# Pinning a DRAM clearing among a GNN layer's loads, and issuing the next layer's edge gathers behind the expert scatters

## The chip, the cores and the metric

The kernel runs on one core of a Trainium2 chip. The metric is device time in microseconds (us) of one execution, the median of several. The engines are named as the profile names them: PE (TensorE, matmuls, with its weight loads as PEld), DVE (VectorE), ACT (ScalarE), POOL (GpSimd) and SP (SyncE, which here only issues DMAs). SPq and ACTq are the DMA issues of SP and ACT.

## The reference, cut to what matters

A graph of 3125 nodes with 256 features and 100,000 edges sorted by `dst` passes through two layers:

```
xn = layernorm(x)
x  = x + gnn0(xn, edges) + linear_attention0(xn)      # layer 0: two rounds of (x + mean of neighbours) @ W
x  = x + moe0(layernorm(x))                           # 8 experts, each node goes to its top 2
xn = layernorm(x)
x  = x + relational_attention(xn, edges, edge_type)   # layer 1: softmax over each node's edges
       + linear_attention1(xn)
x  = x + moe1(layernorm(x))                           # 6 experts, top 2
```

The change touches two pieces of preparation. The first is the table into which the tokens of `moe0` are sorted by expert, and which must hold zeros where no token comes. The second is the reading of the edge lists (`dst`, `src`, `edge_type`) in the order in which layer 1 wants them.

## The kernel before

The work goes through these stages, with times of the profiled execution:

- **Start (0 to 75 us).** `x` is loaded by ACT's queue (`xs`). `Places` (L919) finds where each window of edges begins: it makes row numbers `wrow_i` (L954), gathers 400 KB of `dst` rows six times through two buffers `rw` (L958), and counts in each on DVE (L960). `Windows` (L982) gathers ten windows of 128 KB (`win_dst`, `win_src`, L994) and turns them into the classes `val_a` and `val_s`.
- **Counts (75 to 368 us).** `Counts` (L1604) builds the adjacency matrix of edge counts in DRAM, in 79 groups: one-hots `oh_a` and `oh_s` on DVE (L1619), matmuls (L1634), a cast to `adj_o` on ACT (L1635, six buffers), and a store by SP (L1636, 250 KB from 125 partitions). The linear attention of layer 0 is woven in by hand.
- **Two GNN layers (375 to 925 us).** For each group of columns (512 nodes, the last ones smaller) five loads `at` of the adjacency (L2169, 640 KB each, four buffers, SP's queue) feed the matmuls of L2180. After a group of the second layer, `Routes.tokens` (L1821) picks the two experts of each node, computes the rows `slot` on DVE (L1905), and POOL scatters the nodes' rows into the DRAM table `route_x` (L1909), two DMAs for each tile of 128 nodes, 50 in all.
- **Experts (964 to 1500 us).** `experts` (L1974) takes 32 steps: 8 for the first 256 rows of each expert and 24 for what is left over. Each step loads 256 rows `fx` from `route_x` (L1993) and the weights, transposes (`ftp`, L2013), scales on DVE (`fxe`, L2015), multiplies (`fhp`, L2030; `fyp`, L2038) and stores `route_y`. After each step it calls `beside(s)`, in which other work is placed between the steps.
- **Layer 1 (1500 us to the end).** A table of projected rows is written, then 831 gathers from it feed the attention over edges, and the last experts follow.

Two things stand beside these stages. `Routes.clear` (L1815) writes zeros over `route_x`: 104 DMAs of 256 KB by SP, from a tile `zero`. In the program's text it is called four DMAs at a time after each `at` load of the first GNN layer, from its second group on:

```
for _ in range(4 if layer == 0 and c else 0):
    next(clear, None)
```

`Blocks` (L1030) prepares the edges of layer 1: 75 gathers on POOL (L1048, 25 each for `dst`, `src` and `edge_type`, each 128 rows of 34 numbers), and then `finish`, a generator of steps, the first of which reads `dst`, the second `rel`, the third `rel` and `src`. `beside(s)` takes one of these steps after each expert step from step 8 on, and starts the load of `wn` (L2243, eight DMAs on POOL's queue) at step 16, for the first use at step 22.

The order of instructions on an engine is not always that of the text. A scheduler places them, and where an instruction's inputs are ready early it may be moved ahead. In stretches under `manual_schedule` the text's order holds: in the counts for all engines, in the experts only for the engines in `ORDERED` (L916: PE, DVE and ACT). SP and POOL are not in it. So, in this kernel, SP's queue holds 68 clears ahead of the first adjacency store and the other 36 among the first stores, and POOL's queue holds 14 of the edge gathers ahead of the four scatters of the 23rd and 24th tile, and 17 more between these and the two scatters of the last, the 25th.

`tc.keep_in_program_order(ins)` ties an instruction behind everything written before it for its engine, as an order of issue; it adds no wait.

Of the kernel before, what the change touches and what calls it, by code (L numbers as in the profile page):

```python
# [9 lines left out]
I32 = mybir.dt.int32  # L10
# [7 lines left out]
P = 128  # L18
NB = 25
# [389 lines left out]
def run_all(steps):  # L409
    for _ in steps:  # L410
        pass
# [493 lines left out]
BO = [sum(BW[:b]) for b in range(NB + 1)]  # L905
# [124 lines left out]
class Blocks:  # L1030
# [3 lines left out]
    def __init__(self, nc, keep, dram, pool, a, places):  # L1034
        k = lambda shape, dt, name: keep.tile(shape, dt, name=name)
        t = lambda shape, dt, name: pool.tile(shape, dt, name=name)
        n = BO[NB]
        self.at = k([P, n], I32, "b_at")
        self.dl = k([P, n], F32, "b_dl")
        self.rel = k([P, n], BF, "b_rel")  # L1040
        self.found = k([P, 1], F32, "b_found")
        self.order = dram.tile([n, P], BF, name="b_order")
        self.raw = raw = {}
        for name, src in (("dst", "dst"), ("src", "src"), ("rel", "edge_type_8")):
            raw[name] = t([P, n], I32, "b_" + name)
            flat = a[src].rearrange("(e o) -> e o", o=1)
            for b in range(NB):
                nc.gpsimd.indirect_dma_start(  # L1048
                    out=raw[name][:, BO[b]:BO[b + 1]], out_offset=None, in_=flat,
                    in_offset=bass.IndirectOffsetOnAxis(ap=places.blocks[:, b:b + 1], axis=0))  # L1050

    def finish(self, nc, C, dram, pool, ps):

# [81 lines left out]
class Layer1:  # L1135
# [50 lines left out]
    def load(self, A, c):  # L1186

        if c >= A["n"]:
            return
        k = min(CW, A["w"] - c * CW)  # L1190
        i = A["c0"] + c * CW
        oe = self.wk.tile([P, CW * P], BF, name="oe", bufs=3)
        self.nc.sync.dma_start(oe[:, :k * P], self.B.order[i:i + k, :].rearrange("c e -> (c e)")[None, :]
                               .to_broadcast([P, k * P]))
        A["oe"][c] = oe
# [596 lines left out]
class Routes:  # L1792
# [19 lines left out]
        nc.vector.memset(self.ones, 1.0)  # L1812
        self.tiles = t([1, 2, NT], I32, "route_tiles")

    def clear(self, nc, z):  # L1815

        for i in range(0, NE0 * XR, 2 * P):
            nc.sync.dma_start(self.x[i:i + 2 * P, :].rearrange("(p a) d -> p (a d)", p=P), z)  # L1818
            yield

    def tokens(self, tc, C, wk, ps, xs, t0, nt, wr, br):  # L1821
# [223 lines left out]
def score_weights(nc, C, a, late, f, wn, blk_p):  # L2045

    at_w = f.tile([P, 2, 2 * HD], F32, name="at_w")
    head = f.tile([P, 2, HD], F32, name="head")
    for oc in range(2):
        nc.vector.tensor_scalar(head[:, oc, :], C.row[:, :HD], float(-4 * oc), C.pd[DH],  # L2050
                                op0=OP.add, op1=OP.is_equal)
    for i, name in enumerate(("L1_gnn_attn_srcc", "L1_gnn_attn_dstc")):
        col = f.tile([P, 2], F32, name=f"att{i}")
        nc.sync.dma_start(col, a[name])
        for oc in range(2):
            nc.vector.tensor_scalar(at_w[:, oc, i * HD:(i + 1) * HD], head[:, oc, :],
                                    col[:, oc:oc + 1], None, op0=OP.mult)

    score_w = late.tile([P, 2, 2 * R * HD], F32, name="score_w")
    sp = blk_p.tile([P, 2, R, 2 * HD], F32, name="sp", tag="w")  # L2060
    for r in range(R):
        for k in range(2):
            for oc in range(2):
                nc.tensor.matmul(sp[:, k, r, :], wn[:, r, oc, k * P:(k + 1) * P], at_w[:, oc, :],
                                 start=(oc == 0), stop=(oc == 1))
    for k in range(2):
        nc.vector.tensor_copy(score_w[:, k, :R * HD].rearrange("p (r h) -> p r h", r=R),
                              sp[:, k, :, :HD])
        nc.vector.tensor_copy(score_w[:, k, R * HD:].rearrange("p (h r) -> p r h", r=R),
                              sp[:, k, :, HD:])  # L2070
    return score_w
# [3 lines left out]
def fast(ctx: ExitStack, tc: tile.TileContext, a, out, flag):  # L2075
    nc = tc.nc
# [14 lines left out]
    T_ = Routes(nc, C, keep, dram)  # L2091
# [8 lines left out]
    zero = nodes.tile([P, 2 * D], F32, name="zero")  # L2100
    nc.vector.memset(zero, 0.0)
    nc.scalar.dma_start(gam, row_bc(a["L0_mix_gamma"], D))
    with tc.tile_pool(name="a_sb", bufs=1) as a_sb, tc.tile_pool(name="a_ps", bufs=2, space=PSUM) as a_ps, \
# [3 lines left out]
        with tc.tile_pool(name="find", bufs=1) as find:  # L2107
            places = Places(nc, C, keep, find, a_ps, a)
# [34 lines left out]
    with tc.tile_pool(name="g", bufs=1) as g1, tc.tile_pool(name="ga", bufs=4) as ga, \  # L2143
# [4 lines left out]
        br = g1.tile([P, NE0], F32, name="br")  # L2148
        nc.scalar.dma_start(br, row_bc(a["L0_ffn_br"], NE0))
        rdeg = g1.tile([P, NP], F32, name="rdeg")  # L2150
        clear = T_.clear(nc, zero)
        for t in range(0, NB, 2):
            mix.result(t, mix_p, gt, gam, xs)
        py = nodes.tile([P, 3, NB, D], BF, name="py", tag="late")
# [1 line left out]
        for layer, parts in enumerate((px, py)):  # L2156
# [5 lines left out]
            for c, cw in (GROUPS if layer == 0 else GROUPS1):  # L2162
                agg = [gg.tile([P, 512], F32, name=f"agg{g}") for g in range(2)]
                sums = rdeg[:, c:c + cw]
                for kb in range(NB // KB):
                    at = ga.tile([P, KB, 512], BF, name="at")
                    k0 = kb * KB
                    m = KB if k0 + KB < NB else KB - 1
                    nc.sync.dma_start(at[:, :m, :cw], adj[k0 * P:(k0 + m) * P, c:c + cw].rearrange(  # L2169
                        "(k p) s -> p k s", p=P))  # L2170
                    if m < KB:
                        nc.sync.dma_start(at[:LAST, m, :cw], adj[full:N, c:c + cw])
                    for _ in range(4 if layer == 0 and c else 0):
                        next(clear, None)
                    for i in range(KB):
                        k = k0 + i
                        n = P if k < NB - 1 else LAST
                        for g in range(2):
                            for j in range(3):
                                nc.tensor.matmul(agg[g][:, :cw], parts[j][:n, k, g * P:(g + 1) * P],  # L2180
                                                 at[:n, i, :cw], start=(k == 0 and j == 0),
                                                 stop=(k == NB - 1 and j == 2))
                        if layer == 0 and k > 0:
                            nc.vector.tensor_tensor(sums[:n, :], at[:n, i, :cw],
                                                    at[:n, 0, :cw] if k == 1 else sums[:n, :], OP.add)
# [25 lines left out]
                for i in range(nt):  # L2211
                    t = c // P + i
                    z = gt.tile([P, D], F32, name="z")
# [17 lines left out]
    with tc.tile_pool(name="blk", bufs=1) as blk, tc.tile_pool(name="blk_p", bufs=1, space=PSUM) as blk_p, \  # L2231
            tc.tile_pool(name="f", bufs=1) as f:
        B_ = Blocks(nc, late, dram, blk, a, places)

        score_w = None
        wn = f.tile([P, R, 2, D], F32, name="wn")
        steps = B_.finish(nc, C, dram, blk, blk_p)

        def beside(s):
            nonlocal score_w  # L2240
            if s == 16:
                for r in range(R):
                    nc.gpsimd.dma_start(wn[:, r], a["L1_gnn_W"][r].rearrange("(k p) n -> p k n", p=P))  # L2243
            if s == 22:
                score_w = score_weights(nc, C, a, late, f, wn, blk_p)
            if s >= 8:
                next(steps, None)
            if s < NE0 + NT - 1:
                return
            run_all(steps)  # L2250

            ok = blk.tile([P, 1], F32, name="ok")
            nc.vector.memset(ok, 1.0)
            tot = blk_p.tile([1, 1], F32, name="tot", tag="w")
            nc.tensor.matmul(tot, found_w, ok, start=True, stop=False)
            nc.tensor.matmul(tot, B_.found, ok, start=False, stop=True)
            nc.vector.tensor_scalar(flag, tot, float(2 * E), None, op0=OP.not_equal)

        T_.results(nc, C, blk)
        with tc.tile_pool(name="fw", bufs=2) as fw, tc.tile_pool(name="fk", bufs=3) as fk, \  # L2260
                tc.tile_pool(name="fp", bufs=2, space=PSUM) as fp:
            with tc.manual_schedule(engines=ORDERED):
                experts(tc, C, T_, a, f, fw, fk, fp, beside)


    with tc.tile_pool(name="n1", bufs=1) as n1:
# [7 lines left out]
        with tc.tile_pool(name="r", bufs=1) as r1, tc.tile_pool(name="rw", bufs=3) as rw, \  # L2274
# [21 lines left out]
            for t in range(NB):  # L2296
                for i in range(2):
                    y = rw.tile([P, D], F32, name=f"y{i}")
                    nc.gpsimd.indirect_dma_start(  # L2299
                        out=y, out_offset=None, in_=T_.y,  # L2300
                        in_offset=bass.IndirectOffsetOnAxis(ap=T_.back[:, i * NB + t:i * NB + t + 1], axis=0))
# [22 lines left out]
                ap = rp.tile([P, 2 * R * HD], F32, name="ap", tag="b")  # L2324
# [8 lines left out]
                n = P if t < NB - 1 else LAST  # L2333
# [34 lines left out]
@with_exitstack  # L2368
def gps_two_layers(ctx: ExitStack, tc: tile.TileContext, a, out):
    nc = tc.nc  # L2370
    hold = ctx.enter_context(tc.tile_pool(name="hold", bufs=1))
    flag = hold.tile([1, 1], I32, name="flag")
    fast(tc, a, out, flag)
    with tc.If(nc.values_load(flag[0:1, 0:1], min_val=0, max_val=1) > 0):
        general(tc, a, out)
# [51 lines left out]
```

## Time and profile before

| | us |
|---|---|
| median of 3 runs | 3091.99 |
| lowest and highest | 3090.39, 3094.61 |
| the profiled execution's own time | 3668.28 |
| its span in the profile | 3666.3 |
| PE busy in the span | 2620.8 (71%) |
| DVE busy | 1834.4 (50%) |
| POOL busy | 1061.8 (29%) |
| ACT busy | 738.1 (20%) |

The profiled execution is slower than the others by 576 us, so its span is not the metric, and stretches of it have to be carried over with care. A line of the profile names the engine, the line of the kernel, the operation and the tiles (`out<-in`); the idle time of the engine just before, and what ended it, stand in square brackets in a timeline. A row of a table of windows has the stretch, its length, then for PE, PEld, DVE, ACT and POOL the busy time and the number of instructions, the clock granted to PE, the mean busy share of the 16 DMA engines and the GB/s that they moved. DMA issues on SP, ACT and POOL end with the issue; the data lands later.

### The profile page before, as it was taken

The page shows a single profiled execution, that of the slowest core. Times are in us where ns is not written, and L with a number is a line of the kernel's source. Part 1 is how long each engine was busy: PE and PEld are TensorE (multiplying, and loading weights), DVE is VectorE, ACT ScalarE, POOL GpSimd, SP SyncE. Part 2 cuts the span into 40 slices and gives each one's busy share as a digit, 9 for nine tenths or more (in the row PEclk, how much of TensorE's full clock was granted, in tenths as well). Part 3 has the DMA queues.
Part 4 walks back from the last instruction along what each step waited for, and adds up shares of the span by engine and source line. Part 5 has one row for each costly group of instructions (what it writes and reads, how often), then busy time and mean ns, then how long its engine had stood idle before and what let it go on. Part 6 is the DMA issues. An engine that isn't in the chain of part 4 may idle for free.

```text
span 3666.3 us, 38085 instructions
## 1 busy us (share of the span) xinstructions
PE 2620.8 (71%) x13535; PEld 1774.6 (48%) x13535; DVE 1834.4 (50%) x4049; ACT 738.1 (20%) x1637; POOL 1061.8 (29%) x1040
## 2 busy tenths in 40 slices
PE   2787999998189999799454337637736746845778
PEld 1565545456178888444233324434424533533556
DVE  6898877565111111476315444454545544544552
ACT  3444121222022222232100011111101101101122
POOL 1000000012710000310324644644543554554500
PEclk9899999999589999899776668968867877977989
DMA  8533322332256656443423333433432342343322
GB/s 297 153 84 74 93 84 77 97 98 85 66 171 191 188 170 186 154 144 126 147 71 82 104 94 98 117 90 98 114 100 78 104 123 83 106 123 84 105 58 82
DMA packets 382414, 421.67 MB, mean 115 GB/s; under 512 B 143878, under 2 KB 316044, under 8 KB 381958
## 3 DMA queue, kind: packets, MB, share of 16 engines
q1 hardware_dynamic: 311680, 270.61, 24.4%
q0 software_dynamic: 49072, 132.49, 13.0%
q10 hardware_dynamic: 21462, 16.03, 1.4%
q8 instruction: 109, 1.79, 0.2%
q14 instruction: 91, 0.75, 0.1%
HBM read 321.04 MB, written 97.96 MB: 114 GB/s over the span
## 4 chain that ended last, share of the span: by engine, by line
PE 50%; another core or an unknown queue 18%; DVE 15%; issue 8%; DMA 4%; ACT 2%; POOL 2%; SPq 1%; ACTq 0%; DVEq 0%; POOLq 0%
PE agg L2180 8%; PE fhp L2030 6%; PE fyp L2038 6%; PE sums L1468 6%; PE hp L2318 5%; PE hp L1270 4%; PE yp L1322 3%; DVE r L1454 2%; PE hp L2202 1%; DVE oh_a L1619 1%; DVE oh_s L1619 1%; SPq L1818 1%; PE cnt L1634 1%; PE kvp L2336 1%
## 5 line engine op out<-in xcount | busy, mean ns | idle before, releaser
L1383 POOL DMA_INDIRECT r<-tab,b_at x831 | 865.8, 1042 | 1049.5 <-PE tp L1524 472.1
L1468 PE MATMUL sums<-r,oh 128*128 128x264 f32 x1662 | 436.5, 420 | 78.5 <-DVE oh L1457 60.0
L1214 PE MATMUL dp<-a,ot 128*128 128x64 bf16 x2493 | 116.5, 210 | 485.6 <-DVE own L1225 320.7
L1468 PEld LDWEIGHTS sums<-r,oh 128*128 128x128 f32 x1662 | 343.3, 209 | 165.5 <-issue 60.3
L1214 PEld LDWEIGHTS <-ot 128*128 128x128 bf16 x2493 | 108.3, 109 | 512.6 <-issue 416.1
L1909 POOL DMA_INDIRECT route_x<-x,slot x50 | 50.4, 1007 | 802.1 <-DVE slot L1905 649.7
L1225 DVE TENSOR_TENSOR own<-dp,orel 128x512 f32<-128x512 f32 (+1 forms) x122 | 74.1, 607 | 401.7 <-remote 331.9
L2030 PE MATMUL fhp<-fxe,fw 128*128 128x256 f32 x1024 | 239.3, 392 | 45.6 <-issue 19.2
L1454 DVE TENSOR_TENSOR r<-r 128x1792 f32<-128x1792 f32 (+2 forms) x123 | 240.5, 1955 | 0.0
L2030 PEld LDWEIGHTS fhp<-fxe,fw 128*128 128x128 f32 x1024 | 189.7, 195 | 89.0 <-issue 21.5
L1322 PE MATMUL yp<-ew,h 128*128 128x256 f32 x600 | 168.2, 431 | 89.0 <-DVE xs L1326 86.4
L1273 ACT ACTIVATE h<-hp,bc 128x512 f32<-128x512 f32 (+2 forms) x168 | 105.4, 639 | 622.2 <-PE hp L1270 322.8
L2038 PE MATMUL fyp<-fw,fhid 128*128 128x256 f32 x1024 | 228.0, 381 | 0.0
L2180 PE MATMUL agg<-at,py 128*128 128x512 bf16 (+4 forms) x1200 | 219.6, 336 | 1.4 <-issue 1.3
L2180 PE MATMUL agg<-at,px 128*128 128x512 bf16 (+2 forms) x1050 | 217.6, 358 | 0.8 <-DMA row_b<-in_L_gnn_b 0.8
L2038 PEld LDWEIGHTS fyp<-fw,fhid 128*128 128x128 f32 x1024 | 193.4, 191 | 25.3
L2299 POOL DMA_INDIRECT y<-route_y,slot x50 | 50.0, 1001 | 509.1 <-DMA wq<-in_L_mix_wqT 481.7
L2318 PE MATMUL hp<-wt,xt 128*128 128x512 f32 x400 | 184.4, 609 | 12.1 <-ACT stage L2323 6.0
L2031 ACT ACTIVATE fhid<-fhp,fb 128x256 f32<-128x256 f32 x256 | 121.3, 474 | 324.0 <-PE fhp L2030 280.3
L1322 PEld LDWEIGHTS yp<-ew,h 128*128 128x128 f32 x600 | 124.5, 216 | 127.2 <-DVE xs L1326 96.5
L1270 PE MATMUL hp<-xt,ew 128*128 128x512 f32 (+2 forms) x336 | 165.6, 617 | 17.5 <-ACT h L1273 11.6
L1270 PE MATMUL hp<-h,ew 128*128 128x512 f32 (+2 forms) x336 | 159.6, 601 | 1.5 <-issue 1.5
(419 smaller groups left out, 3834.6 us busy)
## 6 DMA issues: line engine op xcount, KB each, us to landing
fw<-in_L_ffn_W SPq DMA_DIRECT2D x64, 1024.0 KB
ew<-in_L_ffn_expert_w SPq DMA_DIRECT2D x126, 256.0 KB
at<-adj SPq DMA_DIRECT2D x44, 640.0 KB
route_x<-zero SPq DMA_DIRECT2D x104, 256.0 KB
tab<-stage SPq DMA_DIRECT2D x25, 1056.0 KB
oe<-b_order SPq DMA_DIRECT2D x97, 256.0 KB
adj<-adj_o SPq DMA_DIRECT2D x78, 250.0 KB
r<-tab,b_at POOLq DMA_INDIRECT x831
```

Source lines behind the costliest of these rows:

```text
L1214: nc.tensor.matmul(dp[:, i, :, :].rearrange("p h r -> p (h r)"), ot[:, i * P:(i + 1) * P], A["a3"][:, j, :], start=(j == 0), stop=(j == 2))
L1270: nc.tensor.matmul(hp[:, :W], ws[i, e][:, n, j * P:(j + 1) * P], x[:, n, :W], start=(n == 0), stop=(n == 1))
L1273: nc.scalar.activation(o[:, j, :W], hp[:, :W], AF.Relu, bias=b[:, e, j:j + 1])
L1322: nc.tensor.matmul(yp, h2[e][:, n, i * P:(i + 1) * P], ws[3, e][:, n, :], start=(n == 0), stop=(n == 1))
L1383: st = self.nc.gpsimd.indirect_dma_start(out=r[:, c, :], out_offset=None, in_=self.table, in_offset=bass.IndirectOffsetOnAxis(ap=self.B.at ...
L1454: nc.vector.tensor_tensor(rv, rv, r[:, :k, D:, None].to_broadcast([P, k, HD, DH]), OP.mult)
L1468: mm = nc.tensor.matmul(self.sums, oh[:, c, :], r[:, c, :], start=(i == 0), stop=(i == w - 1))
L2030: nc.tensor.matmul(hp, w1[:, k, i * P:(i + 1) * P], xe[:, k, :], start=(k == 0), stop=(k == 1))
L2031: nc.scalar.activation(hid[:, i, :], hp, AF.Gelu, bias=b1[:, 0, i:i + 1])
L2038: nc.tensor.matmul(yp, hid[:, i, t * P:(t + 1) * P], w2[:, i, :], start=(i == 0), stop=(i == K1 - 1))
L2180: nc.tensor.matmul(agg[g][:, :cw], parts[j][:n, k, g * P:(g + 1) * P], at[:n, i, :cw], start=(k == 0 and j == 0), stop=(k == NB - 1 and j ...
L2318: nc.tensor.matmul(hp.rearrange("p r d -> p (r d)"), xt[:, k, :], wt[:, k, j * 512:(j + 1) * 512], start=(k == 0), stop=(k == 1))
```

## The change

- `Routes.clear` issues its DMAs with `keep_in_program_order`, so that they stay among the `at` loads after which they are written.
- The 75 gathers move out of `Blocks.__init__` into a generator `load`. It takes the gathers by fives. Ahead of each five, DVE writes zeros over the part of the tile that the five fill, so that the gathers wait for this memset. Each `next(loads)` issues one memset and five gathers.
- `beside(s)` calls `next(loads)` twice after each of the expert steps 0 to 7, which takes all 15 fives.
- The gathers and the loads of `wn` are issued with `keep_in_program_order`.

In the instruction order of the changed kernel PE and ACT have the same rows as before. DVE has fifteen memsets more (three to a tile of 151 numbers a row, the others 170), at the steps 0 to 7. POOL has all 50 scatters, then the 75 gathers, then the eight loads of `wn`. SP has all stores of the adjacency, then the `at` loads with four clears behind each, beginning with the first load of the second column group.

```diff
         self.order = dram.tile([n, P], BF, name="b_order")
-        self.raw = raw = {}
+        self.raw = {name: t([P, n], I32, "b_" + name) for name in ("dst", "src", "rel")}
+        self.places = places
+
+    def load(self, tc, a):
+
         for name, src in (("dst", "dst"), ("src", "src"), ("rel", "edge_type_8")):
-            raw[name] = t([P, n], I32, "b_" + name)
             flat = a[src].rearrange("(e o) -> e o", o=1)
-            for b in range(NB):
-                nc.gpsimd.indirect_dma_start(
-                    out=raw[name][:, BO[b]:BO[b + 1]], out_offset=None, in_=flat,
-                    in_offset=bass.IndirectOffsetOnAxis(ap=places.blocks[:, b:b + 1], axis=0))
+            raw = self.raw[name]
+            for b0 in range(0, NB, 5):
+                tc.nc.vector.memset(raw[:, BO[b0]:BO[b0 + 5]], 0)
+                for b in range(b0, b0 + 5):
+                    tc.keep_in_program_order(tc.nc.gpsimd.indirect_dma_start(
+                        out=raw[:, BO[b]:BO[b + 1]], out_offset=None, in_=flat,
+                        in_offset=bass.IndirectOffsetOnAxis(ap=self.places.blocks[:, b:b + 1], axis=0)))
+                yield
...
-    def clear(self, nc, z):
+    def clear(self, tc, z):
 
         for i in range(0, NE0 * XR, 2 * P):
-            nc.sync.dma_start(self.x[i:i + 2 * P, :].rearrange("(p a) d -> p (a d)", p=P), z)
+            tc.keep_in_program_order(
+                tc.nc.sync.dma_start(self.x[i:i + 2 * P, :].rearrange("(p a) d -> p (a d)", p=P), z))
             yield
...
+        loads = B_.load(tc, a)
         steps = B_.finish(nc, C, dram, blk, blk_p)
 
         def beside(s):
             nonlocal score_w
             if s == 16:
                 for r in range(R):
-                    nc.gpsimd.dma_start(wn[:, r], a["L1_gnn_W"][r].rearrange("(k p) n -> p k n", p=P))
+                    tc.keep_in_program_order(nc.gpsimd.dma_start(
+                        wn[:, r], a["L1_gnn_W"][r].rearrange("(k p) n -> p k n", p=P)))
             if s == 22:
                 score_w = score_weights(nc, C, a, late, f, wn, blk_p)
-            if s >= 8:
+            if s < 8:
+                for _ in range(2):
+                    next(loads, None)
+            else:
                 next(steps, None)
```

More of the change, by code (lines that the diff above doesn't have):

```diff
@@ L2150, in fast @@
         rdeg = g1.tile([P, NP], F32, name="rdeg")
-        clear = T_.clear(nc, zero)
+        clear = T_.clear(tc, zero)
         for t in range(0, NB, 2):
```

## The prediction

> **What bounds the kernel now.** I read the page's slices first, for the stretches in which PE (TensorE) isn't full; then a table of 10 us windows for the start; then POOL's (GpSimd's) timeline and the chain of waits for the hole near 930 us. The slices:
>
> ```profile
> PE   2787999998189999799454337637736746845778
> DMA  8533322332256656443423333433432342343322
> GB/s 297 153 84 74 93 84 77 97 98 85 66 171 191 188 170 186 154 144 126 147 71 82 104 94 98 117 90 98 114 100 78 104 123 83 106 123 84 105 58 82
> ```
>
> A slice is 92 us. PE is idle in slice 1 while DMA is at its busiest of the whole run; it is full through both GNN layers (slices 5 to 10) and through the experts (12 to 16), with a hole at slice 11. The edit touches these two holes and the full stretches beside them. The start in windows (PE, PEld, DVE, ACT, POOL busy, clock, DMA share, GB/s):
>
> ```profile
> 10.00:20.00 10.00, 0.79 (x2) 0.50 (x2) 9.34 (x62) 0.69 (x1) 0.83 (x1) 1.00 1.07 397
> 30.00:40.00 10.00, 1.68 (x7) 0.87 (x5) 4.76 (x12) 3.55 (x11) 1.89 (x2) 1.00 1.02 365
> 60.00:70.00 10.00, 0.46 (x4) 0.38 (x5) 4.35 (x6) 0.05 (x1) 1.22 (x2) 1.00 1.04 398
> 70.00:80.00 10.00, 6.15 (x39) 4.43 (x38) 6.73 (x16) 8.48 (x29) 0.00 (x0) 1.00 0.09 35
> ```
>
> The DMA engines are saturated until 70 us and then empty, and compute starts exactly there: 68 of the 104 clears (256 KB each, 17.8 MB) are issued from 1.9 to 69.0 us. The rest of the clears sit between the adjacency stores until 160 us. Now POOL at the hole:
>
> ```profile
> 933.61 0.97 POOL L1909 DMA_INDIRECT route_x<-x,slot  x1 [0.30 <-issue]
> 934.88 1.07 POOL L1048 DMA_INDIRECT b_dst<-in_dst,bstart_i  x1 [0.30 <-issue]
> ...
> 955.01 0.94 POOL L1048 DMA_INDIRECT b_src<-in_src,bstart_i  x1 [0.30 <-issue]
> 956.25 1.58 POOL L1909 DMA_INDIRECT route_x<-x,slot  x1 [0.30 <-issue]
> 958.14 1.57 POOL L1909 DMA_INDIRECT route_x<-x,slot  x1 [0.31 <-issue]
> ```
>
> The last two scatters stand behind 17 gathers of layer 1's edges, and the first expert's load of `fx` (SP's timeline: 964.08) waits for all scatters. In the chain of waits these gathers are links. PE then takes this:
>
> ```profile
> 966.94 1.09 PE L2013 MATMUL ftp<-ident,fx 128*128 128x128 f32 x4 [28.58 <-DMA fx<-route_x]
> 987.04 1.22 PE L2030 MATMUL fhp<-fxe,fw 128*128 128x256 f32 x2 [19.01 <-DVE fxe L2015]
> 1028.78 8.76 PE L2038 MATMUL fyp<-fw,fhid 128*128 128x256 f32 x32
> ```
>
> Between 928 and 1028 something else is seen: every engine but POOL moves in small steps. Dependent DVE (VectorE) instructions start some 1.4 us apart (0.2 us at 926), and step 0's first half takes 41 us against 7.2 us in step 1. I call this **the crawl**. I hold most of it for a cost of profiling: the profiled execution takes 3668.28 us (span 3666.3), the median of the unprofiled runs is 3091.99. PE is busy 2620.8 us, so it idles 1045 us in the profile and at most 471 us without. The windows put about 724 us of the idle time into 1800 to 3500 us and some 80 us into 925 to 1030, the two stretches in which POOL issues long rows of gathers; the other 241 us can't supply the 574 us that vanish.
>
> **What the Trainium skill says.** "DMA: Bandwidth & Descriptors", Issuing engines are not separate DMA queues: DMAs of any issuer share the same 16 engines and interleave. The trace agrees: with SP's clears running, POOL's gathers of `rw` (400 KB) were used 6.0, 5.2, 5.6, 5.1 and 6.0 us after their issue ended. The same page, Anatomy of one DMA, fits a GpSimd DMA as 2.0 us + bytes/436e3, so 2.9 us for 400 KB and 2.3 us for a window of 128 KB; these are my estimates for an unloaded start, and no run here shows them yet. "Perfetto Trace Analysis", DMA Instruction — SWDGE: the profiled end is that of descriptor generation, not of the data. So the 0.95 us + 0.30 us of a gather are POOL's own time, not hidden by idle DMA engines. The DMA page again, Why a DMA increments its semaphore by 16: an HWDGE DMA uses the largest number of engines up to 16 that divides both slowest dimensions. The adjacency store has 125 partitions, so 5 engines; at 200 to 350 us, with it alone, the share is 0.32 to 0.38 (5 of 16 is 0.31). Agreed.
>
> **The change part by part.**
>
> *1. Clears leave the start.* The instruction order of the changed kernel has all 104 clears on SP behind the stores, four behind each adjacency load (`at`) from layer 0's second column group on. The start loses 17.8 of some 25.7 MB. (a) DVE waits 2.62 + 1.75 us for `xs` before it can make `wrow_i` at 18.73; with 3.2 MB alone on the engines, I take 2.6 us of it back. (b) The six `rw` gathers go in three pairs, two buffers. DVE idles 2.68 + 3.46 + 0.38 + 2.54 + 1.30 = 10.4 us for them; with 2.9 us instead of 6.0, 5.2 and 5.1 us a pair, 3.1 + 2.3 + 2.2 = 7.6 us come back. (c) The window gathers: one took 2.58 us instead of 0.95 on POOL (1.6 us), and the last was used 4.3 us after its issue, estimated at 2.3 (2.0 us): 3.6 us. Sum 13.8 us; I take **14**. Bounds: 7, if latency stays near 4 us; 20, as DVE idles some 29 us before 75 us and part of that is dependency.
>
> *2. Clears leave the stores.* From 138 to 160 us the chain of waits runs through clears and stores on SP's queue:
>
> ```profile
> 138.42 3.93 SPq L1818 DMA_DIRECT2D route_x<-zero  x2
> 142.45 0.31 SPq L1636 DMA_DIRECT2D adj<-adj_o  x1
> 142.80 4.79 SPq L1818 DMA_DIRECT2D route_x<-zero  x2
> 147.68 0.30 SPq L1636 DMA_DIRECT2D adj<-adj_o  x1
> ```
>
> Six `adj_o` buffers fill and ACT (ScalarE) waits 17.6 us for stores. But DVE, the fuller engine here (46.0 of 50 us in 150 to 200), idles only 2.61 + 2.37 us for it. I take **4**; bounds 0 and 7.
>
> *3. Clears enter layer 0.* A group of five `at` loads takes SP 39.5 us (487.52 to 527.00), 7.9 us a round, or 6.9 us at PE's fastest (30 matmuls of 0.23). A round moves 640 KB; layer 0 ran at 79 to 89 GB/s with a share of 0.26 to 0.31, so 290 GB/s at full share, 2.3 us. Four clears (1.05 MB) at the start's 365 GB/s take 2.9 us, and SP issues them in under 4 us. Sum 5.2 us in 6.9, and four `at` buffers give three rounds of slack. PE's matmuls hide it, and it can't gain, since PE is full there: **0**. The first scatter is at 711 us, after layer 0's end near 642, so the clears are done. Cost if the cover fails: the first rival.
>
> *4. Gathers leave the scatters.* POOL's order now has all 50 scatters first, then 75 gathers, then the 8 `wn` loads. From `own` to the last `slot` the previous tiles took 3.3 us (917.17 to 920.48); from the last `top_eq` at 927.27 I count 0.9 us to `own`, so `slot` is ready at 931.5 without the crawl. The scatters start then, instead of at 956.25: **24 us**. `fx`, transposes and `fxe` follow as before. Lower bound 16 (17 gathers at 0.94, no gaps). Upper bound: the crawl is real and goes too; PE's steady pace then starts at about 942 instead of 1021 (1028.8 less 7.8), 79 us.
>
> *5. Gathers enter the experts' steps.* Fifteen memsets of 128x170 on DVE: the 128x256 one took 0.27 us, so 0.2 us each, 0.4 a step; DVE is busy 7 to 10 of 50 us there. Two fives a step are 12.5 us of POOL in a step of 14.35 us; POOL has nothing else, and only `wn` stands behind. The last five follow step 7's memset, end 6.3 us later and land 2 us after; their first reader is step 9. `wn` is read at step 22. On the DMA engines the gathers alone took a share of 0.11 (985 to 1014 us), beside the experts' 0.58. The weights are two-buffered. PE hides all, and with PE full there is no gain to be had: **0**; bounds 0 and 77 (94 us of POOL time at the crawl's loss of 0.82).
>
> Sum: 14 + 4 + 24 = 42 us. Against the profiled execution's own 3668.28 us, with the crawl's 55 us gone from the gap too: 3668 - 42 - 55 = 3571. Without profiling the crawl is left out: 3092 - 42 = **3050 us**.
>
> **The rivals.** *Layer 0 turns DMA-bound (slower).* `at` and clears share SP's queue. At the 130 to 160 GB/s of 110 to 160 us, where clears alternated with stores, a round of 1.7 MB takes 11.3 us instead of 7.9; 26 rounds cost 88 us, net 3138. It decides from 9.5 us a round (180 GB/s), where 26 x 1.6 eats the 42 us. For it: SP was held 2 us a clear there. Against: the stores were held on 5 engines, `at` isn't.
>
> *The crawl is real.* Then the gap gives 79 instead of 24, total 97: 2995. If it returns in the experts' steps (up to 77 us), about 3072.
>
> *The start is dependency, not bandwidth.* Part 1 gives little and part 4 its lower bound: 3092 - 18 = 3074.
>
> *It doesn't bite:* the scatters wait for `slot` anyway and the cover in layer 0 costs what the start gives: 3088 to 3095. Against: 17 gathers stand in front by POOL's own timeline.
>
> **How the numbers follow.** The likeliest case 0.62 (3050, own range 3030 to 3070); the crawl partly or wholly real 0.12 (2995 to 3030, or 3072); a dull start 0.10 (3074); no bite 0.06; layer 0 or the experts slowed to a net loss 0.10. A measurement of this kernel can tell about 0.2%, 6 us. Faster 0.84, same 0.06, slower 0.10. The range 3015 to 3085 leaves out the loss and the largest gains.
>
> **What would show it.** Right: the first `oh_a` near 61 us instead of 75; DMA share well under 1 before 60 us; no waits of `adj_o` for stores; layer 0 still 267 us from 375 to 642 with PE full; the last scatter 24 us or more nearer to the last `top_eq`; expert steps of 14.35 us. Wrong: PE waiting for `at` in layer 0, steps 0 to 7 longer than the later ones, or the first `fx` no nearer to layer 1's end.

## The result, and the profile after

| | median us | runs | lowest, highest |
|---|---|---|---|
| before | 3091.19 | 4 | 3087.27, 3094.61 |
| after | 3056.51 | 4 | 3054.46, 3056.87 |

The ratio is 0.9886, with a 95% interval of 0.9871 to 0.9901: 34.7 us (1.1%) faster. The prediction was 3050, faster.

The profiled execution of the changed kernel took 3056.87 us (span 3054.8): it isn't slowed as that of before was. Its slices (one is 76 us here, 92 us before):

```profile
PE   2788799999978999996999764688787978869888
...
DMA  3333456533335766564533644554555545454412
GB/s 110 74 70 72 107 187 206 179 99 104 96 115 160 225 194 188 164 193 155 164 123 126 176 119 114 144 149 124 158 141 148 155 126 159 135 154 141 137 45 85
```

The first slice moves 110 GB/s where it moved 297, slices 6 to 8 (layer 0) move 179 to 206 where there were 77 to 93 in that stage, and from the expert steps on the engines don't stand still as they did. The start in the same windows as before (PE, PEld, DVE, ACT, POOL busy, clock, DMA share, GB/s):

```profile
10.00:20.00 10.00, 0.79 (x2) 0.50 (x2) 10.00 (x66) 1.19 (x1) 2.07 (x2) 1.00 0.62 195
30.00:40.00 10.00, 4.24 (x14) 2.33 (x14) 8.50 (x28) 5.88 (x18) 2.85 (x3) 1.00 0.25 85
60.00:70.00 10.00, 7.03 (x38) 4.58 (x36) 6.44 (x14) 7.21 (x25) 0.00 (x0) 1.00 0.00 1
70.00:80.00 10.00, 3.66 (x18) 2.01 (x17) 10.00 (x28) 8.76 (x29) 0.00 (x0) 0.77 0.12 27
```

The DMA share is 0.62 and 0.25 where it was 1.07 and 1.02; PE and ACT are already at work at 60 to 70 us. In DVE's timeline these are all the waits that are left for the gathers of `rw`, then the one for `win_src`; the last line is the first one-hot:

```profile
21.50 1.05 DVE L960 SCALAR_TENSOR_TENSOR junk<-rw,wkey,ones 128x800 f32<-128x800 int32 x1 [1.17 <-DMA rw<-in_dst,wrow_i]
...
23.56 1.05 DVE L960 SCALAR_TENSOR_TENSOR junk<-rw,wkey,ones 128x800 f32<-128x800 int32 x1 [0.69 <-DMA rw<-in_dst,wrow_i]
...
26.56 1.05 DVE L960 SCALAR_TENSOR_TENSOR junk<-rw,wkey,ones 128x800 f32<-128x800 int32 x1 [0.37 <-DMA rw<-in_dst,wrow_i]
...
28.81 1.05 DVE L960 SCALAR_TENSOR_TENSOR junk<-rw,wkey,ones 128x800 f32<-128x800 int32 x1 [0.85 <-DMA rw<-in_dst,wrow_i]
...
34.00 1.05 DVE L960 SCALAR_TENSOR_TENSOR junk<-rw,wkey,ones 128x800 f32<-128x800 int32 x1 [0.75 <-DMA rw<-in_dst,wrow_i]
...
52.93 0.83 DVE L1006 TENSOR_SCALAR wpart<-win_src 128x1280 int32<-128x1280 int32 x1 [4.61 <-DMA win_src<-in_src,wstart_i]
...
62.21 1.23 DVE L1626 TENSOR_TENSOR oh_a<-row_b,val_a 128x2048 bf16<-128x2048 bf16 x1 [2.80 <-PE vt L1021]
```

The five waits for `rw` sum to 3.8 us where they were 10.4; `wpart` comes at 52.93 (65.80 before), and `oh_a` at 62.21 (75.09). POOL at the other hole:

```profile
916.27 1.56 POOL L1917 DMA_INDIRECT route_x<-x,slot  x1 [5.94 <-DVE route_at L1912]
918.14 1.84 POOL L1917 DMA_INDIRECT route_x<-x,slot  x1 [0.30 <-DVE pl_ex L1948]
946.95 0.99 POOL L1054 DMA_INDIRECT b_dst<-in_dst,bstart_i  x1 [26.97 <-ACT fhid L2039]
...
960.64 0.94 POOL L1054 DMA_INDIRECT b_dst<-in_dst,bstart_i  x1 [1.45 <-DVE b_dst L1052]
```

The last two scatters stand alone, 3.7 and 5.6 us behind the last `top_eq` (912.54), and the gathers come in tens behind the memsets of the expert steps. PE takes it up:

```profile
926.89 1.09 PE L2021 MATMUL ftp<-ident,fx 128*128 128x128 f32 x4 [11.79 <-DMA fx<-route_x]
928.61 3.76 PE L2038 MATMUL fhp<-fxe,fw 128*128 128x256 f32 x8 [0.64 <-DVE fxe L2023]
...
938.30 7.07 PE L2046 MATMUL fyp<-fw,fhid 128*128 128x256 f32 x32
945.21 7.17 PE L2038 MATMUL fhp<-fxe,fw 128*128 128x256 f32 x32
...
959.56 7.11 PE L2038 MATMUL fhp<-fxe,fw 128*128 128x256 f32 x32
```

`ftp` waits 11.79 us for `fx` instead of 28.58, `fxe` costs 0.64 instead of 19.01 (which belongs to the crawl: the second profile of before, below, has 0.64 as well), and from step to step `fhp` starts 14.35 us apart (945.21, 959.56) although ten gathers run beside each.

### The profile page after: what moved, and what is told of

Read it like the earlier page. It is cut to its first block, busy times and chain, and to the rows that moved or that the text cites. A ratio compares the mean times of both kernels' runs of the same rounds, so it can differ in the third digit from the quotient of the medians.

```text
span 3054.8 us, 38070 instructions
## 1 busy us (share of the span) xinstructions
PE 2555.2 (84%) x13493; PEld 1742.3 (57%) x13535; DVE 1835.2 (60%) x4064; ACT 738.6 (24%) x1637; POOL 1121.3 (37%) x1040
## 4 chain that ended last, share of the span: by engine, by line
PE 61%; DVE 18%; DMA 7%; POOL 6%; issue 5%; ACT 2%; ACTq 0%; DVEq 0%; SPq 0%; POOLq 0%
PE agg L2188 9%; PE fhp L2038 7%; PE sums L1475 7%; PE fyp L2046 7%; PE hp L1277 7%; POOL r L1390 5%; PE hp L2331 5%; PE yp L1329 4%; DMA r<-tab,b_at 2%; DVE oh_a L1626 2%; DVE oh_s L1626 2%; PE hp L2210 2%; DMA at<-adj 2%; PE cnt L1641 1%; PE kv L1734 1%
## 5 line engine op out<-in xcount | busy, mean ns | idle before, releaser
L1390 POOL DMA_INDIRECT r<-tab,b_at x831 | 926.7, 1115 | 487.7 <-issue 227.0
L1475 PE MATMUL sums<-r,oh 128*128 128x264 f32 x1662 | 427.4, 413 | 43.2 <-DVE oh L1464 24.7
L1475 PEld LDWEIGHTS sums<-r,oh 128*128 128x128 f32 x1662 | 336.7, 205 | 127.9 <-issue 50.8
L1329 PE MATMUL yp<-ew,h 128*128 128x256 f32 x600 | 157.5, 412 | 71.9 <-DVE xs L1333 71.3
L2188 PE MATMUL agg<-at,py 128*128 128x512 bf16 (+5 forms) x1181 | 215.8, 334 | 0.9
L1329 PEld LDWEIGHTS yp<-ew,h 128*128 128x128 f32 x600 | 117.8, 206 | 107.7 <-DVE xs L1333 84.3
L1221 PE MATMUL dp<-a,ot 128*128 128x64 bf16 x2493 | 108.2, 205 | 81.6 <-DVE own L1232 45.8
L1277 PE MATMUL hp<-xt,ew 128*128 128x512 f32 (+2 forms) x336 | 158.6, 598 | 15.4 <-ACT h L1280 13.7
L2188 PEld LDWEIGHTS <-py 128*128 128x128 bf16 (+1 forms) x1200 | 111.6, 100 | 88.3 <-issue 5.3
L2023 DVE TENSOR_SCALAR fxe<-ftp,flng,flnb 128x256 f32<-128x256 f32 x64 | 31.9, 539 | 210.3 <-PE ftp L2021 168.4
```

What stands on the lines that cost most here:

```text
L1221: nc.tensor.matmul(dp[:, i, :, :].rearrange("p h r -> p (h r)"), ot[:, i * P:(i + 1) * P], A["a3"][:, j, :], start=(j == 0), stop=(j == 2))
L1277: nc.tensor.matmul(hp[:, :W], ws[i, e][:, n, j * P:(j + 1) * P], x[:, n, :W], start=(n == 0), stop=(n == 1))
L1329: nc.tensor.matmul(yp, h2[e][:, n, i * P:(i + 1) * P], ws[3, e][:, n, :], start=(n == 0), stop=(n == 1))
L1390: st = self.nc.gpsimd.indirect_dma_start(out=r[:, c, :], out_offset=None, in_=self.table, in_offset=bass.IndirectOffsetOnAxis(ap=self.B.at ...
L1475: mm = nc.tensor.matmul(self.sums, oh[:, c, :], r[:, c, :], start=(i == 0), stop=(i == w - 1))
```

## The experiments

The two profiles alone can't divide the 34.7 us, since that of before is slowed. So parts of the change were run by themselves, and the kernel before was profiled again. Stages are compared by three marks in each trace: the first `oh_a`, the first and last matmul of `agg` with `px` (layer 0), and from the last `top_eq` to the first `ftp`.

**The kernel before, profiled again.**

> The kernel before, once more, for a second profile. If the crawl is a matter of that one profiled execution (the profiles of the other kernels have shown none, one with the gathers in their old place among them), the span is about 3090, the first expert steps take 14.35 us, and the last scatter stands about 29 us behind the last top_eq. If the kernel before crawls under the profiler whenever it runs, the span is above 3600 again.

It took 3090.97 us, span 3088.9. POOL and PE at the hole:

```profile
943.67 0.95 POOL L1048 DMA_INDIRECT b_src<-in_src,bstart_i  x1 [0.30 <-issue]
944.92 1.58 POOL L1909 DMA_INDIRECT route_x<-x,slot  x1 [0.30 <-issue]
946.81 1.57 POOL L1909 DMA_INDIRECT route_x<-x,slot  x1 [0.30 <-issue]
```

```profile
955.47 1.09 PE L2013 MATMUL ftp<-ident,fx 128*128 128x128 f32 x4 [37.00 <-DMA fx<-route_x]
957.20 3.78 PE L2030 MATMUL fhp<-fxe,fw 128*128 128x256 f32 x8 [0.64 <-DVE fxe L2015]
...
967.77 7.07 PE L2038 MATMUL fyp<-fw,fhid 128*128 128x256 f32 x32
```

The last `top_eq` is at 915.97, so the last scatter stands 30.8 us behind it and `ftp` 39.5; no engine crawls. The slow stretches belonged to that one profiled execution and not to the kernel; what caused them there stays open. This profile replaces it in what follows.

**The clears alone.** The kernel before, with

```diff
-            nc.sync.dma_start(self.x[i:i + 2 * P, :].rearrange("(p a) d -> p (a d)", p=P), z)
+            tc.keep_in_program_order(
+                tc.nc.sync.dma_start(self.x[i:i + 2 * P, :].rearrange("(p a) d -> p (a d)", p=P), z))
```

> The kernel before, with only the clears pinned behind the loads of layer 0; the edge gathers stay among the scatters. Theory: the counts end 15.3 us earlier (12.9 in the start, 2.4 among the stores), and the four column groups of layer 0 that carry a full load of clears take 40.8 us instead of 39.5, 4.5 us in all: 10.8 us faster than before, about 3080. Rival 1, the longer layer 0 is an accident of the two profiled executions: 15 us faster, 3076, with groups of 39.5 us. Rival 2, the gap behind layer 1 holds more than the 25 us that its profile shows and the clears are worth next to nothing: within 4 us of before.

3080.63 against 3092.43 us of before measured beside it, ratio 0.9966 (0.9953 to 0.9978): 11.8 us by the medians. The first `oh_a` is at 62.51, and layer 0 takes 271.0 us (266.2 in the second profile of before), so rival 1 falls; the hole stays, 30.8 us from `top_eq` to the last scatter.

**The gathers alone.** The changed kernel, with the clears not pinned:

```diff
-            tc.keep_in_program_order(
-                tc.nc.sync.dma_start(self.x[i:i + 2 * P, :].rearrange("(p a) d -> p (a d)", p=P), z))
+            nc.sync.dma_start(self.x[i:i + 2 * P, :].rearrange("(p a) d -> p (a d)", p=P), z)
```

> The changed kernel with its clears not pinned, so that they are issued at the start and among the stores as before; only the gathers are moved. Theory: the last scatter comes 25 us closer to the last top_eq, all of it falls to the end: 24 to 25 us faster than before, about 3067; layer 0's groups take 39.5 us. Rival, the crawl of the profile of before is partly real in plain executions: more than 30 us faster, below 3061. Rival, the gathers beside the expert steps cost something: under 20 us faster, and steps 0 to 7 longer than 14.35 us.

3066.37 us, ratio 0.9919 (0.9892 to 0.9945): 26.1 us by the medians. From the last `top_eq` to `ftp` it is 14.4 us instead of 39.5, and layer 0 takes 265.7 us. The two parts add to 37.9 us; the whole change gives 34.7 in one set of runs and 35.6 in another, within the scatter of such medians.

**The gathers without pacing.**

```diff
-                tc.nc.vector.memset(raw[:, BO[b0]:BO[b0 + 5]], 0)
...
-            if s < 8:
-                for _ in range(2):
-                    next(loads, None)
-            else:
+            if s >= 8:
                 next(steps, None)
...
-        loads = B_.load(tc, a)
+        run_all(B_.load(tc, a))
```

> The changed kernel without the fifteen memsets and without the two fives a step: all 75 gathers stand right behind the last scatter on POOL. Theory: POOL has nothing else to do and PE hides it, so the pacing is worth nothing: within 3 us of the changed kernel, 3054 to 3060. Rival, a long row of gathers slows the other engines in plain executions too (the crawl): the first six or seven expert steps become longer, and 94 us of gathers cost 10 us or more, above 3066.

3058.07 us, ratio 0.9891 (0.9863 to 0.9919): the same as the changed kernel. POOL issues the 75 gathers in one row from 920.01 to 1013.4, and `fhp` still starts every 14.3 us (945.65, 959.99). The order behind the scatters is what matters; the memsets and the fives are worth nothing measurable.

**The clears among the stores instead of layer 0's loads**, first two behind each of 52 stores, then one behind each of the 79 (and the rest one behind a load of layer 0). The edit of the first, in its main lines:

```diff
...
                 counts.count(g)
+                for _ in range(2):
+                    next(clear, None)
...
-                    for _ in range(4 if layer == 0 and c else 0):
-                        next(clear, None)
```

> The changed kernel, with two clears behind each of the first 52 stores of the adjacency instead of four behind each load of layer 0. Theory: layer 0's groups fall back from 40.8 to 39.5 us, 4.5 us; the stores use 5 of 16 DMA engines, so a clear of 256 KB finds room, and with two clears in each 3.5 us (150 GB/s) the adj_o buffers don't fill: 0 to 2 us lost there. 2 to 5 us faster than the changed kernel, 3052 to 3055. Rival, the stores pay for clears as layer 0's loads do: no faster than the changed kernel, 3056 or more, with ACT waiting for adj_o.

> The changed kernel with one clear behind each of the 79 stores of the adjacency, and the other 25 one behind a load of layer 0 each. Two clears a store made the counts 49 us longer, 0.94 us a store: a store of 125 partitions uses five DMA engines, 50 KB on each, and two clears put 32 KB more on each of these five, so 82 KB took 4.4 us. Theory: the five engines bound the stage; at that rate (18.6 KB a us) a store alone takes 2.7 us and a store with one clear 3.55, against the 3.46 us of a round of the counts: between nothing and 0.1 us a store, 0 to 8 us, and layer 0's groups come down to 39.8 us. 3052 to 3062. Rival, SP is held about 2 us by every clear that stands behind a store, whatever the load of the engines: half of the 49 us for each 52 clears, about 35 us in 79 stores, 3085 or more.

The theory was wrong in both, by far: 3099.76 us, ratio 1.0029 (1.0016 to 1.0041), and 3085.74, ratio 0.9983 (0.9971 to 0.9995). The adjacency's stage grew: from the first `oh_a` to layer 0 it took 346.8 and 323.9 us, against 297.9 in the changed kernel. In the second, ACT waits 40.6 us for the stores to free `adj_o` (none in the changed kernel). Layer 0, free of clears in the first, fell back to 265.8 us. The row of DMA shares over 140 to 160 us (40 slices of 0.5 us), first of the changed kernel, then with one clear a store:

```profile
DMA  4343133333410233333103333330133333324333
```

```profile
DMA  3333379333336943333397333337933333494324
```

A store holds its five engines (0.3) for six or seven slices of a round of seven or eight, 3 to 3.5 of 3.5 to 4 us: they have little room, where I had taken 2.7 us a store. With one clear each the holes are gone, and a round becomes 0.33 us longer; with two it becomes 0.94 us longer. As I read it, an average share of 0.33 hid a resource that was nearly full.

This reading has a rival that isn't excluded. The second run's own rival, that SP is held by every clear behind a store, had said 3085 us or more (though with a stage 35 us longer, and it grew by 26), and SP's queue in that run fits it:

```profile
142.62 3.17 SPq L1826 DMA_DIRECT2D route_x<-zero  x1
145.89 0.28 SPq L1643 DMA_DIRECT2D adj<-adj_o  x1
```

A clear among the stores holds SP 3.3 us there (median of 79), a clear behind a load of layer 0 in the same run 0.5. So SP's queue is as full as the five engines. Whether the full engines are what holds SP, or the holding costs by itself, no run here separates.

**Where the clears have room.** 30 on POOL's queue behind the window gathers, one behind every second store, one behind each load of layer 0. `zeros(how, n)` issues the next `n` clears on POOL's queue (`pool`), or on SP's, pinned (`pin`) or not (`plain`):

```diff
             W_ = Windows(nc, C, a_sb, win, a_ps, a, places)
+            clear = T_.clear(tc, zero)
+            next(clear)
+            zeros("pool", 30)
...
                 counts.count(g)
+                zeros("plain", g % 2)
...
+                    zeros("pin", 1 if layer == 0 else 0)
```

> The changed kernel with the clears where the DMA engines have room: 30 on POOL's queue behind the last window gather (51 us on, where the changed kernel's share is 0.00 to 0.10 until 72 us), one behind every second store (39), one behind each load of layer 0 (35). Theory: each place is under its limit; the first oh_a stays at 62.2 us, the counts lose 0 to 2 us, layer 0's groups take 39.6 to 39.8 us instead of 40.8: 2 to 5 us faster than the changed kernel, 3052 to 3055, the best of all. Rival, any clear beside a stage's own transfers costs in proportion: counts 9 us longer, no faster than 3060.

3064.77 us, ratio 0.9927 (0.9902 to 0.9951): not better than the changed kernel, where the theory had 3052 to 3055. The first `oh_a` stays at 62.23, so the 30 clears on POOL's queue (303 GB/s from 50 to 60 us) are hidden there; but from `oh_a` to layer 0 it is 302.6 us (297.9 in the changed kernel), and layer 0 takes 270.6 us with one clear a load, nearly the 271.1 with four. So layer 0's price isn't proportional to the bytes.

**Twice the clears in layer 0.**

```diff
-            tc.keep_in_program_order(
-                tc.nc.sync.dma_start(self.x[i:i + 2 * P, :].rearrange("(p a) d -> p (a d)", p=P), z))
+            for _ in range(2):
+                tc.keep_in_program_order(
+                    tc.nc.sync.dma_start(self.x[i:i + 2 * P, :].rearrange("(p a) d -> p (a d)", p=P), z))
```

> The changed kernel with every clear issued twice, so that about eight stand behind each load of layer 0. Theory: what the clears cost in layer 0 comes from sharing the DMA engines with the at loads. A round then moves 2.7 MB, at the 400 GB/s of these bursts 6.9 us, and with about 2 us in which the engines stand still between rounds about 9 us, over the round's 7.9: the groups become about 44 us long and PE waits for at; 15 to 25 us slower than the changed kernel, about 3076. Rival, the 1.25 us a group are a fixed cost of having clears there at all (an order of issue, a semaphore): about 3057, groups still near 40.8 us. Rival 1 of the prediction (layer 0 runs at 130 to 160 GB/s with clears in it) would give more than 17 us a round and over 3250.

3061.07 us, ratio 0.9911 (0.9888 to 0.9934). Layer 0 takes 276.1 us: 5.0 more than with 104 clears, for 27 MB more. On SP's queue the clears lie unevenly here, 1 to 14 in a row. The slices reach 316 GB/s. The theory's 15 to 25 us were too many, but the cost isn't fixed either; the prediction's rival of a DMA-bound layer 0 (over 3250 here) falls.

**Which loads the clears stand behind.** The same 104 clears, behind the fourth and fifth load of a group, or behind the first three; and the changed kernel once more beside them:

```diff
-                    for _ in range(4 if layer == 0 and c else 0):
+                    for _ in range((0, 0, 0, 8, 10)[kb] if layer == 0 else 0):
                         next(clear, None)
```

```diff
-                    for _ in range(4 if layer == 0 and c else 0):
+                    for _ in range((7, 7, 7, 0, 0)[kb] if layer == 0 and c else 0):
                         next(clear, None)
```

> The changed kernel with the same 104 clears of the same size in layer 0, but behind the fourth and the fifth load of each column group only (8 and 10), from the first group on. In the changed kernel DVE's sums wait for the first three loads of a group (idle 3.9, 1.7 and 3.4 us ahead of them), and these sums come 4.9 us after the load's issue instead of 4.25; the sums of the fourth and fifth load don't wait. Theory: the clears cost because a load with any clear right behind it lands about 0.6 us later, and only the loads that DVE waits for pass it on, by way of the reciprocal and zt to PE. Then the lag is 4.25 us again, the groups take 39.5 us, and it is 3 to 5 us faster than the changed kernel, about 3052. Rival, the bytes themselves or SP's time for them cost: groups near 40.8 us or longer, since they now come in bunches of 4.6 MB; no faster than the changed kernel.

> The same clears behind the first three loads of each group only, seven behind each, from the second group on. Theory: a lag of 4.9 us or more on the loads that DVE waits for, 7 clears of 1.8 MB running 4.6 us into the next load's 6.7 us: groups of 40.8 to 43 us, as slow as the changed kernel or up to 10 us slower, 3056 to 3066, and 4 us or more slower than with the clears behind the other two loads. Rival (bytes or SP's time): the two placements take the same time.

> The changed kernel once more, on the same chip as the two placements, so that they are compared with it directly: 34 to 36 us faster than before, groups of layer 0 of 40.8 us in its profile.

| clears behind | median us | lowest, highest | ratio to before (95%) | layer 0, us |
|---|---|---|---|---|
| fourth and fifth load | 3049.49 | 3044.01, 3058.47 | 0.9872 (0.9851 to 0.9892) | 266.4 |
| every load (the changed kernel) | 3058.19 | 3053.57, 3065.68 | 0.9902 (0.9882 to 0.9923) | 271.7 |
| first three loads | 3058.06 | 3048.24, 3063.96 | 0.9897 (0.9875 to 0.9919) | 273.7 |

DVE's timeline for one group: the three waits for `at` in the second profile of before, then the changed kernel, then the clears behind the late loads:

```profile
484.48 0.69 DVE L2184 TENSOR_TENSOR rdeg<-at 128x512 f32<-128x512 bf16 x1 [3.23 <-DMA at<-adj]
...
492.87 3.59 DVE L2184 TENSOR_TENSOR rdeg<-at,rdeg 128x512 f32<-128x512 bf16 x5 [1.56 <-DMA at<-adj]
499.52 3.60 DVE L2184 TENSOR_TENSOR rdeg<-at,rdeg 128x512 f32<-128x512 bf16 x5 [3.05 <-DMA at<-adj]
```

```profile
478.46 0.69 DVE L2192 TENSOR_TENSOR rdeg<-at 128x512 f32<-128x512 bf16 x1 [3.90 <-DMA at<-adj]
...
486.90 3.60 DVE L2192 TENSOR_TENSOR rdeg<-at,rdeg 128x512 f32<-128x512 bf16 x5 [1.61 <-DMA at<-adj]
494.06 3.60 DVE L2192 TENSOR_TENSOR rdeg<-at,rdeg 128x512 f32<-128x512 bf16 x5 [3.56 <-DMA at<-adj]
497.58 0.68 DVE L2197 TENSOR_SCALAR rdeg<-deg 128x512 f32<-128x512 f32 x1
498.30 3.35 DVE L2198 RECIPROCAL rdeg<-rdeg 128x512 f32<-128x512 f32 x1
...
502.11 1.28 DVE L2201 TENSOR_TENSOR zt<-agg,rdeg 128x512 f32<-128x512 f32 x2
```

```profile
466.31 0.69 DVE L2192 TENSOR_TENSOR rdeg<-at,rdeg 128x512 f32<-128x512 bf16 x1 [0.57 <-DMA at<-adj]
...
483.67 3.60 DVE L2192 TENSOR_TENSOR rdeg<-at,rdeg 128x512 f32<-128x512 bf16 x5 [1.69 <-DMA at<-adj]
490.11 3.60 DVE L2192 TENSOR_TENSOR rdeg<-at,rdeg 128x512 f32<-128x512 bf16 x5 [2.84 <-DMA at<-adj]
493.63 0.68 DVE L2197 TENSOR_SCALAR rdeg<-deg 128x512 f32<-128x512 f32 x1
494.35 3.35 DVE L2198 RECIPROCAL rdeg<-rdeg 128x512 f32<-128x512 f32 x1
...
498.16 1.28 DVE L2201 TENSOR_TENSOR zt<-agg,rdeg 128x512 f32<-128x512 f32 x2
```

The sums of `rdeg` wait for the first three loads of the next group, and on DVE they stand ahead of the reciprocal from which this group's `zt` is made. In the changed kernel the load before the line at 494.06 was issued at 489.21, 4.85 us earlier, with its four clears behind it:

```profile
489.21 0.38 SPq L2177 DMA_DIRECT2D at<-adj  x1
489.64 2.56 SPq L1826 DMA_DIRECT2D route_x<-zero  x4
```

With the clears elsewhere that lag is 4.26 us, as in the second profile of before (4.29). DVE now waits 0.57 us for the fifth load (466.31), which it did not wait for in the other two. PE's waits for `zt`, and for `h` and `y`, which are made from it, follow. From 380 to 630 us they are (total us, times, longest) in the second profile of before:

```profile
PE tp L344 <- ACT y L2218: 3.8, 5, 1.0
PE hp L2202 <- DVE zt L2194: 1.0, 3, 0.6
```

in the changed kernel:

```profile
PE tp L344 <- ACT y L2226: 5.8, 5, 1.3
PE hp L2210 <- DVE zt L2202: 3.7, 5, 0.8
```

with the clears behind the late loads:

```profile
PE tp L344 <- ACT y L2226: 2.8, 2, 1.6
PE hp L2210 <- DVE h L2212: 1.8, 4, 0.7
PE hp L2210 <- DVE zt L2202: 1.2, 4, 0.6
```

and with the clears behind the first three:

```profile
PE hp L2210 <- DVE zt L2202: 10.3, 5, 2.5
PE tp L344 <- ACT y L2226: 2.6, 2, 1.5
```

The sums are 4.8, 9.5, 5.8 and 12.9 us; their differences from before (4.7, 1.0 and 8.1) are layer 0's (5.5, 0.2 and 7.5) to 1 us. The same bytes cost nothing behind the loads that are hardly waited for (layer 0 266.4 us, before 266.2), 5 us behind every load, and 7 behind the ones that DVE waits for. This shows that layer 0's loss comes through the `at` loads' landing and DVE's sums, and the rival, that the bytes or SP's time for them cost by themselves, falls. The late placement beats both kernels: by the medians it is 44.3 us faster than before and 8.7 us faster than the changed kernel. The trace accounts for 5.3 of these, in layer 0; more than that is not shown, since the ranges of the two overlap and the stretch from the first `ftp` on, the same in these three kernels, took 2121.8 to 2128.6 us in their profiles. What stays open: why one clear behind a load delays it almost as much as four (a lag of 4.7 against 4.85 us).

## Why the prediction was right or wrong

The time, the sign and the likeliest case were right. The sum is some 8 us too good, all in one direction: two terms were too large and a zero was too small, while the largest term was right to about 1 us.

| step | predicted us | measured us |
|---|---|---|
| 1. clears leave the start | -14 | -12.3 |
| 2. clears leave the stores | -4 | about -1 (not told from 0) |
| 3. clears enter layer 0 | 0 | +4.8 |
| 4. gathers leave the scatters | -24 | -25.1 |
| 5. gathers in the expert steps | 0 | 0 |
| sum | -42 | -33.6 (unprofiled: -34.7) |

*Step 1* is the first `oh_a`: 74.7 on average in the three profiles with the old start, 62.4 in the changed kernel's two and the clears-alone run. In the first pair of profiles its parts were 1.8 us for `xs` (predicted 2.6: `wrow_i` at 16.95 instead of 18.73), 8.1 for `rw`, from there to `wstart` at 35.31 instead of 45.16 (7.6), and 3.0 for the windows (3.6). The estimated latencies held: the first `rw` gather, issued by 18.5 us, was used at 21.50, 3.0 us later (estimate 2.9; the others that were waited for took 2.8 to 3.8); the last window gather's 128 KB 2.0 us after its issue ended (2.3). The slow window gather was misread: one of the ten stays slow in every profile, 1.73 to 1.88 us on POOL with the clears away and 1.54 to 2.59 with them, so most of the 1.6 us put down to the clears wasn't theirs.

*Step 2* was mis-sized. From the first `oh_a` to layer 0 it is 300.3, 294.5 and 298.5 us with the clears among the stores, and 297.0 to 299.5 in the six profiles without any (the clears-alone run 288.2, at a granted clock of 0.97 from 80 to 340 us, where the others had 0.91 to 0.93). ACT's waits for the stores are gone, as predicted, but little came of it: 1 us on average with the clears-alone run counted, nothing without it. DVE stays the fuller engine (43.2 of 50 us from 150 to 200 in the changed kernel, 44.9 in the second profile of before); that its progress sets the stage is a reading which no run tests.

*Step 3* is the step that failed. The prediction's "four `at` buffers give three rounds of slack" is true of PE and false of DVE, whose sums take each load as it lands; its "PE's matmuls hide it" left out the path from the load by `rdeg` and `zt` to PE. The three waits of DVE on `at` that the trace of before shows (3.2, 1.4 and 3.1 us in a group; the second profile's are shown above) told of it, and were not read. Four profiles with four clears a load give layer 0 271.0 us on average, three with the clears at the start 266.2. The bandwidth side of the step was right: from the third group on the loads were issued 6.6 to 10.9 us apart, against 6.6 to 10.2 before, and the bursts ran at 400 GB/s.

*Step 4* was right to 1 us: from `top_eq` to `ftp` 39.5 us became 14.2 to 14.7 in the profiles with the gathers moved. Its upper bound, the crawl, is ruled out by the second profile of before, by the unpaced gathers, and by the gathers alone giving 26 and not 79 us.

*Step 5* was right, and more strongly than claimed: even all 75 gathers in one row cost PE nothing. The forecast of 3571 us for the profiled execution was wrong, since it took the crawl elsewhere for part of every profile; the profile after shows none.

Of the rivals, a DMA-bound layer 0, a real crawl and a change that doesn't bite are excluded by the runs; a start of pure dependency is excluded by the 12.3 us.

## What to carry to other kernels

Moving transfers off a saturated stretch pays what that stretch waited; to find what they cost in their new place, look for every engine that reads the loads beside them, not only for the one that is full: an engine that takes each load as it lands has no slack, however many buffers there are. Put such transfers behind the loads that nobody is waiting for. And read a DMA share against the engines that a transfer can use, and against the queue that issues it: for stores on five of sixteen engines 0.33 left little room, and a clear put between them held SP's queue as well.

## What the runs showed of the hardware that was not expected

- One 256 KB clear right behind a 640 KB load delayed the sums on it almost as much as four did (4.7 and 4.85 us after the load's issue, 4.25 without).
- One profiled execution of the kernel before took 3668.28 us; a second took 3090.97, with the same program and no slow stretch.
- 75 indirect gathers in one row on POOL (0.94 us each and 0.30 between) beside a full PE changed nothing in PE's 14.3 us a step.
- A clear of 256 KB held SP's queue 3.3 us (median of 79) behind a store on five engines, and 0.5 us behind a load of layer 0, in the same run.
